# The two ends of a chunked scan: order, loads and engines of its first image and its last unit

## The chip, the cores and the metric

One core of one Trainium2 chip runs the whole program in one launch. The metric is device time in microseconds (us), the median of several executions. The kernel before took 3655.25 us (three runs, 3648.51 to 3655.76).

## What is computed

Two layers on a batch of 32 images with 96 channels of 56 x 56 pixels, all in float32. Layer 0 is a ConvNeXt block: a 7x7 depthwise convolution, layer norm over the channels, a two-layer MLP with GELU, and a residual. Layer 1, the one that the change concerns, is a selective scan along the 3136 pixels of each image:

```python
x = conv5x5_depthwise(x) + conv_b
xs = silu(x).reshape(B, C, L)
dts, Bs, Cs = split(einsum('kd,bdl->bkl', x_proj_w, xs))          # 6, 4, 4 rows
delta = softplus(einsum('dr,brl->bdl', dt_w, dts) + dt_b)
log_dA = maximum(delta * -exp(A_logs), log(1e-9))                 # 4 states per channel
P = exp(cumsum(log_dA))
hs = P * cumsum(delta * Bs * xs / maximum(P, 1e-9))
y = einsum('bdnl,bnl->bdl', hs, Cs) + xs * Ds
```

## The kernel before, in words

The program has four stages that follow each other: the 7x7 convolution, the MLP, the 5x5 convolution (whose result goes to DRAM as `conv2_d`) and the scan. The change is in the scan stage alone (lines 534 to 757).

The scan cuts each image in two chunks of CH = 1568 pixels. A step `k` is one chunk of one image, of which there are 64; two neighbouring images (NI = 2) share a pair `p`, whose tokens `load(p)` (L565) brings in by one DMA. Each step has NG = 3 units: a unit `i` is 32 channels times 4 states, that is 128 partitions of 1568 elements. There are 192 units.

A step's data go this way.

- `delta_in` (L582): TensorE computes the argument of delta for half a chunk, 784 columns. `delta` (L590): ScalarE takes its Softplus. `delta_x` (L596): GpSimd multiplies delta with the tokens. The tile `du` holds both, delta and product, side by side.
- `keep_du` (L601) writes `du` to DRAM (L602), and `spread_du` (L636) reads it back for one unit, each channel repeated on four partitions, into a tile `rep` (L642). SyncE (SP) issues both, as well as `load`.
- `rows_bc`, `rows_out` and `spread` (L604 to L634) make the tiles `bt` and `ct`, B and C of the step on 128 partitions, through TensorE and copies on ScalarE.
- `decay` (L645): three ScalarE activations, L648 (Exp), L649 and L650, turn the delta half of `rep` into the decay. `drive` (L652): GpSimd multiplies the product half by `bt` (L654).
- `scan` (L656): VectorE runs a scan that makes P (L664, out to PSUM), a combined min and multiply (L667), and a second scan for the state `hs` (L671).
- `weigh` (L676): GpSimd keeps the last column for the image's second chunk (L681) and multiplies `hs` by `ct` (L682).
- `gather` (L684): TensorE sums the four states of a channel and adds `xs * Ds` (L688, L695), half a chunk at a time. `store` (L702): ScalarE copies the sum out of PSUM (L705) and issues the output DMA (L706).

Every instruction here is recorded through `pin`, which keeps each engine's work in the order in which the program is written. So the loop at L716 is the schedule: at its index `i` it emits the loads and spreads for later units, the decay of unit i+2, the drive of unit i+1, the scan of unit i, the weighing of unit i-1 and, at every third index, sums and stores of the step that has just ended. The pair's delta work is emitted from the place where `at` is 0 (L738 to L752); for the first pair this is index -8. Softplus and Exp lie in different tables of ScalarE, so each change between them has a table load.

Buffers: 5 `rep` tiles, 4 `du` tiles, 5 `hs` tiles, 3 token tiles, and two pairs of PSUM banks that all matmul results of the stage share.

Of the kernel before, what the change touches and what calls it, by code (L numbers as in the profile page):

```python
# [8 lines left out]
F32 = mybir.dt.float32  # L9
AF = mybir.ActivationFunctionType  # L10
# [4 lines left out]
B, C, H, W = 32, 96, 56, 56  # L15
# [6 lines left out]
N, R = 4, 6  # L22
# [10 lines left out]
CH = 1568  # L33
NI = 2
NCH = L // CH
HT = CH // 2
BK = HT // 2
# [4 lines left out]
DG = C // 3  # L42
NG = 3
# [3 lines left out]
def convnext_then_scan_kernel(  # L47
# [22 lines left out]
    nc = tc.nc  # L70
    pin = tc.keep_in_program_order
# [8 lines left out]
    conv2_d = dram.tile([C, H, B * W], F32, name="conv2_d")  # L80
    du_d = dram.tile([B * NCH, C, 2, CH], F32, name="du_d")
# [30 lines left out]
    dtb_t = column(dtb, C, "dtb_t")  # L112
# [27 lines left out]
    dsm_t = const.tile([C, C], F32, name="dsm_t")  # L140

    with tc.tile_pool(name="prep", bufs=1) as prep, tc.tile_pool(
        name="prep_ps", bufs=1, space=PSUM
# [7 lines left out]
        at = H - 1 - K1 // 2  # L151
# [170 lines left out]
    with tc.tile_pool(name="mlp", bufs=2) as pool, tc.tile_pool(  # L322
        name="mlp_h", bufs=3, space=PSUM
# [95 lines left out]
        parts = groups * 2  # L419
# [19 lines left out]
    with tc.tile_pool(name="c2", bufs=3) as pool, tc.tile_pool(  # L439
        name="c2k", bufs=1  # L440
# [93 lines left out]
    with tc.tile_pool(name="sc", bufs=2) as pool, tc.tile_pool(  # L534
        name="sc_k", bufs=1, space=PSUM
# [7 lines left out]
        steps = B * NCH  # L543
        units = steps * NG
# [10 lines left out]
        HQ = H // NCH  # L555

        def place(k):

            p, i = divmod(k, NI)
            return p // NCH * NI + i, p % NCH  # L560

        def bank_pair(name):
            return psum.tile([128, 2, 512], F32, name=name, tag="bc")

        def load(p):  # L565
            b, q = place(p * NI)
            xt = pool.tile([C, HQ, NI * W], F32, name=f"xs_{p}", tag="xs", bufs=3)
            pin(nc.sync.dma_start(
                xt, conv2_d[:, q * HQ : (q + 1) * HQ, b * W : (b + NI) * W]
            ))  # L570
            xts[p] = xt

        def tokens(k, s, n):

            p, i = divmod(k, NI)
            hh = HQ // n
            return xts[p][:, s * hh : (s + 1) * hh, i * W : (i + 1) * W]

        def half(ps, s):
            return ps[:, s, :BK].rearrange("p (h w) -> p h w", w=W)  # L580

        def delta_in(k, h):  # L582
            pzs[k, h] = bank_pair(f"pz_{k}_{h}")
            for s in range(2):
                pin(nc.tensor.matmul(  # L585
                    half(pzs[k, h][:C], s), lhsT=wd_t, rhs=tokens(k, 2 * h + s, 4),
                    start=True, stop=True,
                ))
# [4 lines left out]
            pin(nc.scalar.activation(o, z, AF.Softplus, bias=dtb_t, scale=1.0))  # L593
            dus[k, h] = du

        def delta_x(k, h):  # L596
            du = dus[k, h]
            d, u = (du[:, i, :].rearrange("p (h w) -> p h w", w=W) for i in range(2))
            pin(nc.gpsimd.tensor_mul(u, d, tokens(k, h, 2)))  # L599

        def keep_du(k, h):  # L601
            pin(nc.sync.dma_start(du_d[k][:, :, h * HT : (h + 1) * HT], dus.pop((k, h))))  # L602

        def rows_bc(k):  # L604

# [15 lines left out]
        def spread(k, kind, h):  # L621

            to, name = ((bts, "bt"), (cts, "ct"))[kind]
            if h == 0:
                to[k] = pool.tile([128, CH], F32, name=f"{name}_{k}", tag=name)
            pk = bank_pair(f"pk_{k}_{kind}_{h}")
            for s in range(2):
                at = 32 * (2 * kind + s)
                rows = slice(at, at + 2 * N)
                pin(nc.tensor.matmul(  # L630
                    pk[:, s, :BK], lhsT=pick_t[rows], rhs=bns[k][rows, h],
                    start=True, stop=True, tile_position=(at, 0),
                ))
            pin(nc.scalar.copy(two(to[k][:, h * HT : (h + 1) * HT]), pk[:, :, :BK]))  # L634

        def spread_du(i):  # L636

            k, g = divmod(i, NG)
            rep = pool.tile([128, 2, CH], F32, name=f"rep_{i}", tag="rep", bufs=5)
            du = du_d[k, g * DG : (g + 1) * DG, :, :]  # L640
            src = bass.AP(du.tensor, du.offset, [du.ap[0], [0, N], [1, 2 * CH]])
            pin(nc.sync.dma_start(rep.rearrange("p i t -> p (i t)"), src))  # L642
            reps[i] = rep

        def decay(i):  # L645

# [29 lines left out]
        def weigh(i):  # L676
            k, g = divmod(i, NG)
            q, col = place(k)[1], k % NI * NG + g
            ht = hss[i]
            if q < NCH - 1:  # L680
                pin(nc.gpsimd.tensor_copy(carry_h[:, col : col + 1], ht[:, CH - 1 : CH]))  # L681
            pin(nc.gpsimd.tensor_mul(ht, ht, cts[k]))  # L682

        def gather(k, h):  # L684

            py = bank_pair(f"py_{k}_{h}")
            for s in range(2):
                pin(nc.tensor.matmul(  # L688
                    half(py[:C], s), lhsT=dsm_t, rhs=tokens(k, 2 * h + s, 4),
                    start=True, stop=False,  # L690
                ))
            for s in range(2):
                cols = slice((2 * h + s) * BK, (2 * h + s + 1) * BK)
                for g in range(NG):
                    pin(nc.tensor.matmul(  # L695
                        py[g * DG : (g + 1) * DG, s, :BK], lhsT=sel_t,
                        rhs=hss[k * NG + g][:, cols], start=False, stop=True,
                        tile_position=(0, g * DG),
                    ))
            pys[k, h] = py  # L700

        def store(k, h):  # L702
            b, q = place(k)
            yt = pool.tile([C, HT], F32, name=f"y_{k}_{h}", tag="y")
            pin(nc.scalar.copy(two(yt), pys.pop((k, h))[:C, :, :BK]))  # L705
            pin(nc.scalar.dma_start(out[b, :, q * CH + h * HT : q * CH + (h + 1) * HT], yt))  # L706
# [9 lines left out]
        for i in range(-12, units + 2):  # L716

            p, at = divmod(i + 8, PER)
            g = i % NG
            if at == 3 and p + 1 < PC:  # L720
                load(p + 1)
            at_unit(i + AHEAD, spread_du)
            if 0 <= p < PC and 2 <= at:
# [6 lines left out]
            if g == 1 and 0 <= (i + 2) // NG < steps:  # L730
# [5 lines left out]
            if g == 2 and 0 <= (i + 4) // NG < steps:  # L736
                rows_bc((i + 4) // NG)
            if 0 <= p < PC and at == 0:  # L738
                for j, h in halves[:2]:
                    delta_in(p * NI + j, h)  # L740
            at_unit(i + 2, decay)
            at_unit(i + 1, drive)
            if g == 2 and 0 <= (i + 4) // NG < steps:
                rows_out((i + 4) // NG)
            if 0 <= p < PC and at == 0:
                for a, (j, h) in enumerate(halves):
                    if a >= 2:
                        delta_in(p * NI + j, h)
                    delta(p * NI + j, h)
            if 0 <= p < PC and 1 <= at <= 4:  # L750
                j, h = halves[at - 1]
                delta_x(p * NI + j, h)  # L752
            at_unit(i, scan)
            if g == 0 and 0 <= after < steps:
                gather(after, 0)
                store(after, 0)
                gather(after, 1)


# [42 lines left out]
```

## Time and profile before

| | |
|---|---|
| median of three runs | 3655.25 us |
| the profiled execution: device time, span | 3655.9 us, 3654.1 us |
| busy: TensorE, VectorE, ScalarE, GpSimd | 3060.6, 2655.5, 2341.0, 1950.5 us |
| first load of tokens issued (L568) | 1856.24 us |
| first scan, second scan, third scan start (L664) | 1896.48, 1913.20, 1922.07 us |
| last scan ends (L671) | 3639.06 us |

Times inside the execution count from the start of its span. A row of the timeline gives the start, the duration, engine and line, the operation, what it writes and reads, and in brackets the idle time of the engine before it with what ended that. "SPq" and "ACTq" are issues of DMAs by SyncE and ScalarE. In the page, the span is cut in 40 slices and each digit is the busy share of an engine in one slice, in tenths. A row of the waits gives engine, line, what it waited for, the microseconds in total, how often, and the longest. "xN" counts instructions.

### The profile page before, as it was taken

The page shows a single profiled execution, that of the slowest core. Times are in us where ns is not written, and L with a number is a line of the kernel's source. Part 1 is how long each engine was busy: PE and PEld are TensorE (multiplying, and loading weights), DVE is VectorE, ACT ScalarE, POOL GpSimd, SP SyncE. Part 2 cuts the span into 40 slices and gives each one's busy share as a digit, 9 for nine tenths or more (in the row PEclk, how much of TensorE's full clock was granted, in tenths as well). Part 3 has the DMA queues.
Part 4 walks back from the last instruction along what each step waited for, and adds up shares of the span by engine and source line. Part 5 has one row for each costly group of instructions (what it writes and reads, how often), then busy time and mean ns, then how long its engine had stood idle before and what let it go on. Part 6 is the DMA issues. An engine that isn't in the chain of part 4 may idle for free. (4 is left out here: it accounts for less than half of the span.)

```text
span 3654.1 us, 46458 instructions
## 1 busy us (share of the span) xinstructions
PE 3060.6 (84%) x17290; PEld 1286.4 (35%) x17290; DVE 2655.5 (73%) x1771; ACT 2341.0 (64%) x2133; POOL 1950.5 (53%) x1241
## 2 busy tenths in 40 slices
PE   7999996899999999899957777777777777777775
PEld 5777774333333333333312222222222222222221
DVE  5666665233333333599949999999999999999998
ACT  3555553333333333577858878888888888888884
POOL 2333332122222222100028999999999999999996
PEclk9999998899999999999966666666666666666666
DMA  5555553455555554699977778877877877878873
GB/s 153 166 167 167 168 168 107 149 162 160 163 163 162 162 160 125 169 281 281 288 232 264 259 253 281 276 257 267 276 260 267 281 245 275 274 244 277 281 258 108
DMA packets 302054, 790.70 MB, mean 216 GB/s; under 512 B 123012, under 2 KB 180164, under 8 KB 277156
## 3 DMA queue, kind: packets, MB, share of 16 engines
q1 hardware_dynamic: 259076, 669.31, 56.7%
q0 software_dynamic: 28416, 79.87, 7.3%
q10 hardware_dynamic: 14336, 38.54, 2.7%
q8 instruction: 137, 2.24, 0.3%
q14 instruction: 89, 0.73, 0.1%
HBM read 551.83 MB, written 235.74 MB: 216 GB/s over the span
## 5 line engine op out<-in xcount | busy, mean ns | idle before, releaser
L682 POOL TENSOR_TENSOR hs<-hs,ct 128x1568 f32<-128x1568 f32 x192 | 673.3, 3507 | 104.8 <-DVE hs L671 93.0
L664 DVE TENSOR_TENSOR_SCAN pv<-rep,pv 128x1568 f32<-128x1568 f32 x192 | 664.5, 3461 | 72.2 <-ACT rep L650 54.2
L654 POOL TENSOR_TENSOR rep<-rep,bt 128x1568 f32<-128x1568 f32 x192 | 674.9, 3515 | 14.6 <-DMA rep<-du_d 14.6
L382 ACT ACTIVATE g<-ph,b1p_t 128x896 f32<-128x896 f32 x336 | 320.5, 1005 | 511.8 <-PE ph L372 511.8
L402 DVE SCALAR_TENSOR_TENSOR o<-po,b2r_t,x 128x224 f32<-128x224 f32 x336 | 190.4, 608 | 572.4 <-PE po L391 572.4
L286 PE MATMUL ps<-xq,wt 120*112 120x448 f32 x1536 | 581.9, 540 | 14.1 <-POOL xq L281 14.1
L414 POOL DMA_DIRECT2D block_d<-o x336 | 183.7, 553 | 703.5 <-DVE o L402 621.3
L286 PEld LDWEIGHTS ps<-xq,wt 120*112 120x112 f32 x1536 | 429.4, 280 | 166.2 <-POOL xq L281 14.3
L372 PE MATMUL ph<-h,w1r_t 32*128 32x448 f32 x4032 | 440.3, 559 | 55.8 <-DVE h L362 54.4
L599 POOL TENSOR_TENSOR du<-du,xs 96x784 f32<-96x784 f32 x128 | 236.3, 1847 | 373.7 <-ACT du L593 373.7
L585 PE MATMUL pz<-xs,wd_t 96*96 96x392 f32 x512 | 277.3, 707 | 172.0 <-ACT du L593 139.1
L391 PE MATMUL po<-g,w_t 128*32 128x448 f32 x4032 | 413.1, 543 | 0.0
L695 PE MATMUL py<-hs,sel_t 128*32 128x392 f32 x1536 | 328.6, 685 | 68.5 <-POOL hs L682 68.5
L630 PE MATMUL pk<-bn,pick_t 8*128 8x392 f32 x1024 | 287.3, 682 | 98.4 <-ACT y L705 78.8
L667 DVE SCALAR_TENSOR_TENSOR pv<-pv,rep 128x1568 f32<-128x1568 f32 x192 | 345.6, 1800 | 21.1 <-POOL hs L682 1.4
L480 PE MATMUL ps<-xq,wt 128*32 128x448 f32 x3072 | 309.9, 548 | 39.3 <-DMA xq<-block_d 36.5
L671 DVE TENSOR_TENSOR_SCAN hs<-rep,carry_h,pv 128x1568 f32<-128x1568 f32 x96 | 334.0, 3479 | 10.4 <-DVE pv L667 0.5
L503 DVE COPY st<-yt 28x896 f32<-28x896 f32 x288 | 317.7, 1103 | 26.9 <-DMA conv_d<-st 13.2
L671 DVE TENSOR_TENSOR_SCAN hs<-rep,pv 128x1568 f32<-128x1568 f32 x96 | 328.4, 3421 | 10.3 <-DVE pv L667 0.9
L688 PE MATMUL py<-xs,dsm_t 96*96 96x392 f32 x512 | 308.6, 746 | 11.7 <-ACT bn L618 6.1
L648 ACT ACTIVATE rep<-rep,a_t 128x1568 f32<-128x1568 f32 x192 | 308.3, 1606 | 11.6 <-DMA rep<-du_d 11.2
L649 ACT ACTIVATE rep<-rep,lift_t 128x1568 f32<-128x1568 f32 x192 | 307.6, 1602 | 6.2
(85 smaller groups left out, 3155.4 us busy)
## 6 DMA issues: line engine op xcount, KB each, us to landing
rep<-du_d SPq DMA_DIRECT2D x192, 1568.0 KB
du_d<-du SPq DMA_DIRECT2D x128, 588.0 KB
xq<-block_d SPq DMA_DIRECT2D x192, 225.0 KB
block_d<-o POOLq DMA_DIRECT2D x336, 120.0 KB, 5.6
xt<-in_x_dram SPq DMA_DIRECT2D x192, 196.0 KB
h<-conv_d SPq DMA_DIRECT2D x84, 448.0 KB
x<-in_x_dram SPq DMA_DIRECT2D x336, 112.0 KB
conv_d<-st SPq DMA_DIRECT2D x96, 392.0 KB
```

What stands on the lines that cost most here:

```text
L286: nc.tensor.matmul(ps[:, j, :PQ].rearrange("p (i r) -> p i r", i=BI), lhsT=wv[:KR, t], rhs=xq[:KR, j, :, t : t + W2], start=(t == 0), stop ...
L372: pin(nc.tensor.matmul(phs[i // 2][:, i % 2, :HALF], lhsT=w1r_t[rows, d, f * 128 : (f + 1) * 128], rhs=hts[n, d][rows, s * HALF : (s + 1) ...
L382: nc.scalar.activation(gt, ph[:, :, :HALF], AF.Gelu, bias=b1p_t[:, f : f + 1], scale=1.0)
L391: pin(nc.tensor.matmul(po[CB * i : CB * i + CB, :HALF], lhsT=w2_t[:, f, CB * d : CB * d + CB], rhs=gts[n, s, f, i // 2][:, i % 2], start=( ...
L480: pin(nc.tensor.matmul(ps[RW * f : RW * f + RW, h, : B * QW].rearrange("p (b q) -> p b q", q=QW), lhsT=wv[:, f, t], rhs=xv[:, :, t : t + Q ...
L503: pin(copy(st[:, :, :, :, f], yt[RW * f : RW * f + QR].rearrange("p h (b q) -> p h b q", q=QW),))
L654: pin(nc.gpsimd.tensor_mul(ut, ut, bts[i // NG]))
L664: pin(nc.vector.tensor_tensor_scan(grown, da, zero, pv[:, last : last + 1] if q else 1.0 / EPS, ALU.mult, ALU.add))
L667: pin(nc.vector.scalar_tensor_tensor(run, in0=grown, scalar=1.0, in1=ut, op0=ALU.min, op1=ALU.mult))
L671: pin(nc.vector.tensor_tensor_scan(ht, da, run, carry_h[:, col : col + 1] if q else 0.0, ALU.mult, ALU.add))
L682: pin(nc.gpsimd.tensor_mul(ht, ht, cts[k]))
L695: pin(nc.tensor.matmul(py[g * DG : (g + 1) * DG, s, :BK], lhsT=sel_t, rhs=hss[k * NG + g][:, cols], start=False, stop=True, tile_position= ...
```

## The change

At the start of the scan, for the first pair:

- The first pair's tokens are loaded by two DMAs, one for each image.
- All that the first image needs is emitted at loop index -8 in an order of its own: a Softplus of one column ahead of everything, delta of both halves, delta alone to DRAM, `rep` of unit 0 with delta alone; after these its product, now on VectorE, to DRAM and into the other half of `rep`; then the load of the second pair, `rep` of units 1 and 2, `bt`, decay and drive of unit 0; then delta, product and store of the second image.
- Decay and drive of unit 1 are emitted at index -2, ahead of the second pair's delta work; decay of unit 2 at index -1.

At the end, for the last unit and the last step:

- The product of `hs` and `ct` is made by VectorE for the first 784 columns and by GpSimd for the others.
- The sums over the first two units, with the `xs * Ds` part, are emitted before the last unit's; only the last unit's matmuls remain after it.
- The second half's copy is made by VectorE and its output DMA is issued by SyncE.

The core of the diff:

```diff
         def load(p):
-            pin(nc.sync.dma_start(
-                xt, conv2_d[:, q * HQ : (q + 1) * HQ, b * W : (b + NI) * W]
-            ))
+            rows = conv2_d[:, q * HQ : (q + 1) * HQ, b * W : (b + NI) * W]
+            for i in range(1 if p else NI):
+                cols = slice(None) if p else slice(i * W, (i + 1) * W)
+                pin(nc.sync.dma_start(xt[:, :, cols], rows[:, :, cols]))
...
-        def delta_x(k, h):
+        def delta_x(k, h, engine=nc.gpsimd):
...
-        def keep_du(k, h):
-            pin(nc.sync.dma_start(du_d[k][:, :, h * HT : (h + 1) * HT], dus.pop((k, h))))
+        def keep_du(k, h, part=slice(0, 2)):
+            pin(nc.sync.dma_start(
+                du_d[k][:, part, h * HT : (h + 1) * HT], dus[k, h][:, part]
+            ))
...
-        def spread_du(i):
+        def spread_du(i, part=slice(0, 2)):
...
-            pin(nc.gpsimd.tensor_mul(ht, ht, cts[k]))
+            if i < units - 1:
+                pin(nc.gpsimd.tensor_mul(ht, ht, cts[k]))
+            else:
+                for engine, cols in (nc.vector, slice(0, HT)), (nc.gpsimd, slice(HT, CH)):
+                    pin(engine.tensor_mul(ht[:, cols], ht[:, cols], cts[k][:, cols]))
...
-        def store(k, h):
+        def store(k, h, copy=nc.scalar.copy, queue=nc.scalar):
...
+            if p == 0 and at == 0:
+                deltas, products = slice(0, 1), slice(1, 2)
+                warm = pool.tile([C, 1], F32, name="warm", bufs=1)
+                pin(nc.scalar.activation(warm, dtb_t, AF.Softplus))
+                for h in range(2):
+                    delta_in(0, h)
+                for h in range(2):
+                    delta(0, h)
+                for h in range(2):
+                    keep_du(0, h, deltas)
+                spread_du(0, deltas)
+                for h in range(2):
+                    delta_x(0, h, nc.vector)
+                    keep_du(0, h, products)
+                rows_bc(0)
+                rows_out(0)
+                spread_du(0, products)
+                load(1)
+                for u in range(1, NG):
+                    spread_du(u)
+                for h in range(2):
+                    spread(0, 0, h)
+                decay(0)
+                drive(0)
+                for h in range(2):
+                    delta_in(1, h)
+                    delta(1, h)
+                    delta_x(1, h)
+                    keep_du(1, h)
+                continue
...
+            ready = {-2: [1], -1: [2], 0: []}.get(i, [i + 2])
+            driven = {-2: [1], -1: [], 0: []}.get(i, [i + 1])
...
+            if i == units - 1:
+                for h in range(2):
+                    gather(steps - 1, h, range(NG - 1))
+            if i == units:
+                for h in range(2):
+                    gather(steps - 1, h, range(NG - 1, NG))
+                store(steps - 1, 0)
+                store(steps - 1, 1, nc.vector.tensor_copy, nc.sync)
```

More of the change, by code (lines that the diff above doesn't have):

```diff
@@ L594, in delta @@
             dus[k, h] = du
-        def delta_x(k, h):
+        def delta_x(k, h, engine=nc.gpsimd):
             du = dus[k, h]
             d, u = (du[:, i, :].rearrange("p (h w) -> p h w", w=W) for i in range(2))
-            pin(nc.gpsimd.tensor_mul(u, d, tokens(k, h, 2)))
-        def keep_du(k, h):
-            pin(nc.sync.dma_start(du_d[k][:, :, h * HT : (h + 1) * HT], dus.pop((k, h))))
+            pin(engine.tensor_mul(u, d, tokens(k, h, 2)))
+        def keep_du(k, h, part=slice(0, 2)):
+            pin(nc.sync.dma_start(
+                du_d[k][:, part, h * HT : (h + 1) * HT], dus[k, h][:, part]
+            ))
         def rows_bc(k):
@@ L634, in spread @@
             pin(nc.scalar.copy(two(to[k][:, h * HT : (h + 1) * HT]), pk[:, :, :BK]))
-        def spread_du(i):
+        def spread_du(i, part=slice(0, 2)):
             k, g = divmod(i, NG)
[L639 to L643, printed above, removed]
+            if i not in reps:
+                reps[i] = pool.tile([128, 2, CH], F32, name=f"rep_{i}", tag="rep", bufs=5)
+            to = reps[i][:, part].rearrange("p i t -> p (i t)")
+            du = du_d[k, g * DG : (g + 1) * DG, part, :]
+            src = bass.AP(du.tensor, du.offset, [du.ap[0], [0, N], [1, to.shape[1]]])
+            pin(nc.sync.dma_start(to, src))
         def decay(i):
@@ L681, in weigh, with gather @@
                 pin(nc.gpsimd.tensor_copy(carry_h[:, col : col + 1], ht[:, CH - 1 : CH]))
[L682 to L691, printed above, removed]
+            if i < units - 1:
[3 more added lines that the diff above has]
+                    pin(engine.tensor_mul(ht[:, cols], ht[:, cols], cts[k][:, cols]))
+        def gather(k, h, parts=range(NG)):
+            if parts[0] == 0:
+                pys[k, h] = bank_pair(f"py_{k}_{h}")
+                for s in range(2):
+                    pin(nc.tensor.matmul(
+                        half(pys[k, h][:C], s), lhsT=dsm_t, rhs=tokens(k, 2 * h + s, 4),
+                        start=True, stop=False,
+                    ))
+            py = pys[k, h]
             for s in range(2):
                 cols = slice((2 * h + s) * BK, (2 * h + s + 1) * BK)
-                for g in range(NG):
+                for g in parts:
                     pin(nc.tensor.matmul(
@@ L699, in gather @@
                     ))
-            pys[k, h] = py
-        def store(k, h):
+        def store(k, h, copy=nc.scalar.copy, queue=nc.scalar):
             b, q = place(k)
             yt = pool.tile([C, HT], F32, name=f"y_{k}_{h}", tag="y")
-            pin(nc.scalar.copy(two(yt), pys.pop((k, h))[:C, :, :BK]))
-            pin(nc.scalar.dma_start(out[b, :, q * CH + h * HT : q * CH + (h + 1) * HT], yt))
+            pin(copy(two(yt), pys.pop((k, h))[:C, :, :BK]))
+            pin(queue.dma_start(out[b, :, q * CH + h * HT : q * CH + (h + 1) * HT], yt))
         def at_unit(i, fn):
@@ L715, in convnext_then_scan_kernel @@
         halves = [(i, h) for i in range(NI) for h in range(2)]
-        for i in range(-12, units + 2):
+        for i in range(-12, units + 1):
             p, at = divmod(i + 8, PER)
             g = i % NG
-            if at == 3 and p + 1 < PC:
+            if p == 0 and at == 0:
[28 more added lines that the diff above has]
+                continue
+            if at == 3 and p + 1 < PC and (p + 1) != 1:
                 load(p + 1)
-            at_unit(i + AHEAD, spread_du)
-            if 0 <= p < PC and 2 <= at:
+            if i + AHEAD >= NG:
+                at_unit(i + AHEAD, spread_du)
+            if 0 < p < PC and 2 <= at:
                 j, h = halves[at - 2]
@@ L729, in convnext_then_scan_kernel @@
                 store(after, 1)
-            if g == 1 and 0 <= (i + 2) // NG < steps:
+            if g == 1 and 0 < (i + 2) // NG < steps:
                 for h in range(2):
@@ L735, in convnext_then_scan_kernel @@
                     spread((i + 1) // NG, 1, h)
-            if g == 2 and 0 <= (i + 4) // NG < steps:
+            if g == 2 and 0 < (i + 4) // NG < steps:
                 rows_bc((i + 4) // NG)
-            if 0 <= p < PC and at == 0:
+            ready = {-2: [1], -1: [2], 0: []}.get(i, [i + 2])
+            driven = {-2: [1], -1: [], 0: []}.get(i, [i + 1])
+            if 0 < p < PC and at == 0 and i != -2:
                 for j, h in halves[:2]:
                     delta_in(p * NI + j, h)
-            at_unit(i + 2, decay)
-            at_unit(i + 1, drive)
-            if g == 2 and 0 <= (i + 4) // NG < steps:
+            for u in ready:
+                if u:
+                    at_unit(u, decay)
+            for u in driven:
+                if u:
+                    at_unit(u, drive)
+            if g == 2 and 0 < (i + 4) // NG < steps:
                 rows_out((i + 4) // NG)
-            if 0 <= p < PC and at == 0:
+            if 0 < p < PC and at == 0:
                 for a, (j, h) in enumerate(halves):
-                    if a >= 2:
+                    if a >= 2 or i == -2:
                         delta_in(p * NI + j, h)
                     delta(p * NI + j, h)
-            if 0 <= p < PC and 1 <= at <= 4:
+            if 0 < p < PC and 1 <= at <= 4:
                 j, h = halves[at - 1]
@@ L753, in convnext_then_scan_kernel @@
             at_unit(i, scan)
-            if g == 0 and 0 <= after < steps:
+            if g == 0 and 0 <= after < steps - 1:
                 gather(after, 0)
```

## The prediction

> **What bounds the kernel now.** I read the page first (busy rows, slices), then the waits of DVE, then the timelines around the scan stage's first and last units, then every L664 start against the end of its decay on L650. Page, parts 1 and 2:
>
> ```profile
> PE 3060.6 (84%) x17290; PEld 1286.4 (35%) x17290; DVE 2655.5 (73%) x1771; ACT 2341.0 (64%) x2133; POOL 1950.5 (53%) x1241
> DVE  5666665233333333599949999999999999999998
> ACT  3555553333333333577858878888888888888884
> POOL 2333332122222222100028999999999999999996
> ```
>
> The whole-span shares mix stages. From slice 21 on, the scan stage, DVE is full, POOL as well, ACT at 8 of 10. The waits of DVE from 1900 us to the end:
>
> ```profile
> DVE pv L664 <- ACT rep L650: 10.4, 4, 7.9
> DVE pv L667 <- POOL hs L682: 1.4, 3, 0.5
> ```
>
> Of 1740 us DVE waits some 12: the stage is a DVE chain of 192 units, about 9.04 us each (1913.20 to 3639.06 for 191). An edit pays only where it starts this chain earlier, avoids a hole in it, or shortens what follows its end. The start, two timelines:
>
> ```profile
> 1856.24 0.31 SPq L568 DMA_DIRECT2D xs<-conv_d  x1
> 1864.23 9.92 PE L585 MATMUL pz<-xs,wd_t 96*96 96x392 f32 x16 [19.06 <-DMA xs<-conv_d]
> 1867.20 1.28 ACT L593 ACT_TABLE_LOAD   x1 [19.14 <-PE pz L585]
> ...
> 1871.36 0.64 SPq L602 DMA_DIRECT2D du_d<-du  x1
> 1872.04 0.61 SPq L568 DMA_DIRECT2D xs<-conv_d  x1
> 1873.15 4.92 SPq L602 DMA_DIRECT2D du_d<-du  x1
> ```
>
> ```profile
> 1883.77 0.55 SPq L642 DMA_DIRECT2D rep<-du_d  x1
> ...
> 1891.58 1.60 ACT L648 ACTIVATE rep<-rep,a_t 128x1568 f32<-128x1568 f32 x1 [11.23 <-DMA rep<-du_d]
> ...
> 1896.46 1.28 ACT L593 ACT_TABLE_LOAD   x1
> 1896.48 3.43 DVE L664 TENSOR_TENSOR_SCAN pv<-rep,pv 128x1568 f32<-128x1568 f32 x1 [43.84 <-ACT rep L650]
> ...
> 1908.30 1.60 ACT L648 ACTIVATE rep<-rep,a_t 128x1568 f32<-128x1568 f32 x1
> ...
> 1913.20 3.43 DVE L664 TENSOR_TENSOR_SCAN pv<-rep,pv 128x1568 f32<-128x1568 f32 x1 [7.92 <-ACT rep L650]
> ```
>
> See two things. The second delta store (1873.15) lies behind the 1.2 MB load of the next pair, so the first rep load leaves only at 1883.77. And ACT puts four Softplus, two ct copies and two table loads between decay 0 and decay 1: 16.7 us from the end of one to the end of the other. The tail:
>
> ```profile
> 3635.58 3.48 DVE L671 TENSOR_TENSOR_SCAN hs<-rep,carry_h,pv 128x1568 f32<-128x1568 f32 x1
> 3639.20 3.48 POOL L682 TENSOR_TENSOR hs<-hs,ct 128x1568 f32<-128x1568 f32 x1 [5.58 <-DVE hs L671]
> 3642.74 2.82 PE L695 MATMUL py<-hs,sel_t 128*32 128x392 f32 x8 [7.55 <-POOL hs L682]
> ...
> 3650.67 0.32 ACTq L706 DMA_DIRECT2D out_dram<-y  x1
> ```
>
> From the last scan's end to the span's end: 3654.1 - 3639.06 = 15.0 us.
>
> **What the Trainium skill says.** (1) "DMA: Bandwidth & Descriptors", Queues, rings and completion order: descriptors of one issuing engine are consumed in ring order. The trace agrees: L602 of 1873.15 waits out the load in front of it (11.1 us is the longest wait of L642 for it). (2) "ScalarE: Activation LUTs", What ACT_TABLE_LOAD costs: 1.283 us, plus a drain of 1.38; the trace shows 1.28 us and no drain of its own. (3) "SBUF — State Buffer", Who interferes with whom: a DVE instruction with two SBUF inputs and a POOL instruction reading SBUF exclude each other, the first keeps the port. The scan reads pv from PSUM, so no scan row shows it; in the first convolution a POOL copy (L281) starts at 301.64, just as DVE's two-input add of 300.65 (1.09 us) ends: it fits.
>
> **Part by part, in the clock of this profile.**
>
> *Load by image.* The load took 8.0 us, its data moving from about 1857.4 to 1863.0 (DMA shares by window). Half the bytes, but the same count of packets at half their size: if a packet's cost is constant, 0 gained; if by bytes, 2.8; a small packet may cost more, so -1. I take 0.6: PE starts at 1863.6. The second half follows, done by about 1869, beside PE work.
>
> *Table load early.* The warm Softplus runs in ACT's idle 19 us; but the second Softplus is set by PE (1869.79, 5.6 after PE's start), so 0 on the path. Deltas end at 1863.6 + 6.5 = 1870.1.
>
> *Deltas ahead.* POOL's product leaves the path, as does the next load. Store of 96x784: priced by the last output store, same size, 3.4 us (3650.67 to 3654.1): 1873.5. Rep load of 0.8 MB: rep 0 took 7.8 us with 2.2 MB (it and the store issued behind); less the 2.4 us fixed part of the xs load that is 5.4, so 2.0 + 2.4 = 4.4, bounds 3.9 and 6: 1878.0. Decay 4.9 (1891.58 to 1896.48): first scan 1882.9, not 1896.48. ACT's copies for bt and its table load are hidden before 1878; without that cover they would cost their excess.
>
> *Products behind.* DVE takes the two products, about 1 us each (96x784; 1.08 for 896 columns on L362), while idle: 0. Two more stores and one more rep load on SP: the stores are issued at 1874 behind the delta rep (its data end near 1877) and land at about 1879.8 (1.6 us of data, 1.2 of completion); the product rep lands 4.4 later at 1884.3, and POOL's drive (3.5) ends at 1888. DVE's L667 waits 1.7 us; unit 0 ends at 1893.3, cost hidden by the next point.
>
> *Load(1) ahead of rep 1.* In SP's ring now stand the product rep (data to 1883.3), load(1) with 5.6 us (its data, as the first load's above), rep 1 with 3.9 us (1.6 MB at the 420 GB/s of the busiest windows), 1.2 us completion: rep 1 lands at 1894. Bounds: 1889 if load(1) could be passed, 1897 if the reps run at the rate of rep 0. This is the new wait; rep 2 and image 1's two stores queue behind it but are needed later. Image 1's two Softplus and two table loads (4.4 us) on ACT end before, at 1887.3. Decay 1 ends 1899; scan 1 at 1899, not 1913.2.
>
> *POOL behind these waits.* Its order is now drive 0, image 1's two products, drive 1, two products of the next pair, then the weighing of unit 0, drive 2. Drive 0 (to 1888) and the two products (1.85 each, to 1891.7) end before rep 1 is there; drive 1 is done at 1897.5, needed by L667 at 1902.4. The weighing waits for ct, whose copies end 10.6 us after decay 1 as they did after decay 0 (1896.46 to the weighing at 1907.12): from 1909.6 it and drive 2 take 7.0, to 1916.6; L667 of unit 2 wants it at 1919.3. Covered by 2.7 us; if scan 2 came earlier than I say, this would be the next limit.
>
> *The Softplus block moves to between decays 1 and 2.* It costs its 16.7 there: scan 2 at 1915.8, not 1922.07: 6.3 left. Then ACT has no lead over DVE. Before, it needed 51.6 us from decay 1's end (1913.16) to decay 7's (1964.78), 4.1 of them waiting (idle before L705 and L634). After, the block without its decay is one more thing in that stretch, 16.7 - 4.9 = 11.8, and there are new waits: bn, its matmuls and bt stand directly ahead of decay 3, and the y and bt copies ahead of decay 6 wait for PE at half clock (0.7 us a matmul). Not in the trace; between 0 and 6, I take 4.2: 51.6 - 4.1 + 11.8 + 4.2 = 63.5. Decay 7 ends at 1899.1 + 63.5 = 1962.6, and unit 7 starts there instead of 1966.72. **Start: 4.1 us earlier**, not 14.
>
> Does ACT hold that? In the trace of before its lead fell to nothing three times (units 43, 139, 151), for instance
>
> ```profile
> 2292.63 3.49 DVE L664 TENSOR_TENSOR_SCAN pv<-rep,pv 128x1568 f32<-128x1568 f32 x1 [0.96 <-ACT rep L650]
> ```
>
> and each time was back at 3.0 to 3.3 us six units later. So no further loss.
>
> *Tail.* Two thirds of the matmuls and all of L688 move ahead, under the last scan. DVE's half product: 0.97 us by the 1.08 of L362; POOL's half: 1.8 (L599's 1.85 at the same width). By the skill they exclude each other; DVE starts 0.05 us earlier, so POOL ends at 3639.06 + 0.1 + 1.0 + 1.8 = +2.9. PE's two matmuls of the second half 1.4 (0.7 each, from 2.82 for four), to +4.4; DVE's copy 1.0 (ACT's takes 0.81), SP's store 3.4: +8.9. **Tail: 15.0 - 8.9 = 6.1 us less**. With no exclusion 6.6; with POOL first 4.8.
>
> Sum: 4.1 + 6.1 = 10.2 us from this execution's own 3655.9: 3645.7. The median shown, 3655.25, is 0.65 less: 3645.0.
>
> **Rivals.**
> A, rep 1 is in time (DMA faster, or less behind it): decay 1 follows the Softplus pair at once, ends at 1892.3, 6.8 us sooner, all the way to unit 7. Start 11, tail 6: 3638. Against it: the packet times above.
> B, the start gives nothing (small packets slow, or ACT's catching up costs 4 us more): the tail alone, 3655.25 - 6.1 = 3649.1. For it: each of the four estimates on this path (packets, store, two reps) has only one row behind it.
> C, slower: ACT becomes the bound for good. The lead is reset to nothing at unit 7; if each pair's Softplus block then outruns ACT's recovery, each of the 31 remaining pairs pays. It decides from 10.2/31 = 0.33 us per pair; at 1 us per pair 3655 + 21 = 3676. For it: ACT at 8 tenths and three bare leads. Against it: the recovery to 3 us, each time.
> That the early path isn't taken at all can be set aside: the order of both programs has the delta store and its rep load ahead of the product, waiting for ACT alone.
>
> **Chances.** The forecast 0.56, A 0.17, B 0.22, C 0.05. Range 3638 to 3652: from A to the tail alone with POOL first and 2 us on top. About 0.2%, 7.3 us, is what a measurement here can tell from no change: faster needs under 3647.9. That is A, most of the forecast and a little of B: 0.71; same 0.25; slower 0.04, C.
>
> **What will show it.** First L664 near 1883 and second near 1899, with a hole before it ended by the rep load; scan 2 near 1916 and unit 7 some 4 us earlier, both released by the decay's last step on ACT; from the last scan's end 8.9 us, POOL's half product starting as DVE's ends. Second scan before 1895 means A; holes ended by ACT at every sixth unit mean C.

## The result

The changed kernel took 3641.78 us (median of 8 runs, 3639.02 to 3648.92), the kernel before, beside it on the same chip, 3653.95 us (8 runs, 3648.51 to 3656.82). The ratio is 0.997, with a 95% interval from 0.9959 to 0.9981: faster by 0.3%, 12.2 us between the medians, 7 to 15 us by the interval. The profiled execution of the changed kernel took 3640.0 us, its span 3638.2 us.

### The profile page after: what moved, and what is told of

Its sections match the earlier page's. It is cut to its first block, busy times and chain, and to the rows that moved or that the text cites. A ratio compares the mean times of both kernels' runs of the same rounds, so it can differ in the third digit from the quotient of the medians.

```text
span 3638.2 us, 46478 instructions
## 1 busy us (share of the span) xinstructions
PE 3049.4 (84%) x17290; PEld 1284.6 (35%) x17290; DVE 2661.9 (73%) x1775; ACT 2345.0 (64%) x2135; POOL 1944.1 (53%) x1239
## 5 line engine op out<-in xcount | busy, mean ns | idle before, releaser
L658 POOL TENSOR_TENSOR rep<-rep,bt 128x1568 f32<-128x1568 f32 x192 | 674.5, 3513 | 381.5 <-DMA rep<-du_d 381.5
L687 POOL TENSOR_TENSOR hs<-hs,ct 128x1568 f32<-128x1568 f32 x191 | 669.4, 3505 | 104.0 <-DVE hs L675 91.0
L668 DVE TENSOR_TENSOR_SCAN pv<-rep,pv 128x1568 f32<-128x1568 f32 x192 | 664.5, 3461 | 47.6 <-ACT rep L654 29.9
L705 PE MATMUL py<-hs,sel_t 128*32 128x392 f32 x1536 | 327.0, 681 | 59.9 <-POOL hs L687 59.7
L671 DVE SCALAR_TENSOR_TENSOR pv<-pv,rep 128x1568 f32<-128x1568 f32 x192 | 345.6, 1800 | 22.2 <-POOL hs L687 1.4
L675 DVE TENSOR_TENSOR_SCAN hs<-rep,carry_h,pv 128x1568 f32<-128x1568 f32 x96 | 334.1, 3480 | 10.8 <-DVE pv L671 0.9
L675 DVE TENSOR_TENSOR_SCAN hs<-rep,pv 128x1568 f32<-128x1568 f32 x96 | 328.4, 3421 | 9.9 <-DVE pv L671 0.5
L652 ACT ACTIVATE rep<-rep,a_t 128x1568 f32<-128x1568 f32 x192 | 308.3, 1606 | 10.0 <-DMA rep<-du_d 9.6
L653 ACT ACTIVATE rep<-rep,lift_t 128x1568 f32<-128x1568 f32 x192 | 307.6, 1602 | 6.2
L654 ACT ACTIVATE rep<-rep,lift_t 128x1568 f32<-128x1568 f32 x192 | 307.6, 1602 | 6.3
```

The lines of the kernel that those rows point to most:

```text
L658: pin(nc.gpsimd.tensor_mul(ut, ut, bts[i // NG]))
L668: pin(nc.vector.tensor_tensor_scan(grown, da, zero, pv[:, last : last + 1] if q else 1.0 / EPS, ALU.mult, ALU.add))
L671: pin(nc.vector.scalar_tensor_tensor(run, in0=grown, scalar=1.0, in1=ut, op0=ALU.min, op1=ALU.mult))
L675: pin(nc.vector.tensor_tensor_scan(ht, da, run, carry_h[:, col : col + 1] if q else 0.0, ALU.mult, ALU.add))
L705: pin(nc.tensor.matmul(py[g * DG : (g + 1) * DG, s, :BK], lhsT=sel_t, rhs=hss[k * NG + g][:, cols], start=False, stop=True, tile_position= ...
```

## The profile after

In the changed kernel the first load of tokens is L571, the stores of delta and product L603, the `rep` loads L647, Softplus L594, the decay L652 to L654, the drive L658, the first scan L668, the combined min and multiply L671, the second scan L675, the product with `ct` L687 and, for the last unit, L690, the last sums L705, the copy of y L714, its DMA L715. The warm Softplus is L734.

The page, busy rows and slices, in the order in which they were shown of before:

```profile
PE 3049.4 (84%) x17290; PEld 1284.6 (35%) x17290; DVE 2661.9 (73%) x1775; ACT 2345.0 (64%) x2135; POOL 1944.1 (53%) x1239
...
DVE  5666665233333333599959999999999999999998
ACT  3555553333333333488868888888888888878884
POOL 2333332122222222100029999999999999999896
```

The work is the same. The 21st digit, the slice in which the scan begins, has gone from 4 to 5 on VectorE and from 5 to 6 on ScalarE, the next from 8 to 9 on GpSimd. Some other digits of ScalarE and GpSimd differ by one as well, in slices whose code is the same, so a slice of 91 us says no more than that. The waits of VectorE from 1900 us to the end:

```profile
DVE pv L668 <- ACT rep L654: 11.8, 6, 7.6
DVE y L714 <- PE py L705: 3.3, 1, 3.3
DVE pv L671 <- POOL hs L687: 1.4, 3, 0.5
```

Waits for the decay add up to 11.8 us in six places, 7.6 of it ahead of the third scan. The chain of 192 units is as unbroken as before. So the time can only have changed ahead of it, in its first units, and behind it. The timeline of the start:

```profile
1850.70 2.11 SPq L571 DMA_DIRECT2D xs<-conv_d  x2
1850.70 1.28 ACT L734 ACT_TABLE_LOAD   x1 [7.70 <-DMA conv_d<-st]
...
1856.45 4.71 PE L586 MATMUL pz<-xs,wd_t 96*96 96x392 f32 x8 [16.51 <-DMA xs<-conv_d]
...
1864.77 0.52 SPq L647 DMA_DIRECT2D rep<-du_d  x1
...
1870.36 1.60 ACT L652 ACTIVATE rep<-rep,a_t 128x1568 f32<-128x1568 f32 x1 [3.01 <-DMA rep<-du_d]
...
1872.46 0.59 SPq L571 DMA_DIRECT2D xs<-conv_d  x1
1873.10 4.94 SPq L647 DMA_DIRECT2D rep<-du_d  x2
...
1875.26 3.43 DVE L668 TENSOR_TENSOR_SCAN pv<-rep,pv 128x1568 f32<-128x1568 f32 x1 [12.15 <-ACT rep L654]
...
1879.92 1.80 DVE L671 SCALAR_TENSOR_TENSOR pv<-pv,rep 128x1568 f32<-128x1568 f32 x1 [1.23 <-POOL rep L658]
...
1886.18 1.60 ACT L652 ACTIVATE rep<-rep,a_t 128x1568 f32<-128x1568 f32 x1 [6.62 <-DMA rep<-du_d]
...
1891.08 3.43 DVE L668 TENSOR_TENSOR_SCAN pv<-rep,pv 128x1568 f32<-128x1568 f32 x1 [5.91 <-ACT rep L654]
...
1907.43 3.43 DVE L668 TENSOR_TENSOR_SCAN pv<-rep,pv 128x1568 f32<-128x1568 f32 x1 [7.57 <-ACT rep L654]
```

Read it from the brackets. ScalarE's second decay (1886.18) stood idle for 6.62 us and was released by the DMA into `rep`: unit 1's copy, issued at 1873.10 behind the second pair's load of 1872.46. That is the new wait. The third scan waits 7.57 us for ScalarE, which has the four Softplus between the second decay and the third. The tail:

```profile
3622.65 3.48 DVE L675 TENSOR_TENSOR_SCAN hs<-rep,carry_h,pv 128x1568 f32<-128x1568 f32 x1
...
3626.16 0.97 DVE L690 TENSOR_TENSOR hs<-hs,ct 128x784 f32<-128x784 f32 x1
3626.27 2.56 POOL L690 TENSOR_TENSOR hs<-hs,ct 128x784 f32<-128x784 f32 x1 [5.59 <-DVE hs L675]
...
3630.48 0.97 DVE L714 COPY y<-py 96x784 f32<-96x784 f32 x1 [3.35 <-PE py L705]
3631.48 0.34 SPq L715 DMA_DIRECT2D out_dram<-y  x1
```

The last scan ends at 3626.13, the last store is issued 5.35 us later, and yet the span ends 12.05 us later, at 3638.2. What fills the rest is not a busy instruction. The line where the program ends shows it (duration in ns as min/median/max, then first start and last start); first the changed kernel, then the kernel before:

```profile
L856 POOLq DRAIN  x3: 34/93/11175, 3626.2 to 3637.9; - x3
L856 SPq DRAIN  x3: 7/7/7, 3634.4 to 3637.7; - x3
```

```profile
L798 POOLq DRAIN  x3: 34/93/12098, 3639.2 to 3653.9; - x3
L798 SPq DRAIN  x3: 7/7/7, 3653.3 to 3653.6; - x3
```

SyncE's first drain stands where its wait for the last store is over. Before, that was 3653.3, and GpSimd's long drain had ended at 3639.2 + 12.1 = 3651.3, hidden. Now the store is over at 3634.4, and GpSimd's drain ends at 3626.2 + 11.2 = 3637.4: it is the last thing to end.

For what follows, the measure is the time from the first load of tokens (the first L571 row and its like), so that what the unchanged stages ahead do drops out. S0, S1, S2, S7 are the starts of the first scan of units 0, 1, 2 and 7; the last two columns are what stands between S7 and the last scan's end, and from there to the span's end.

| profile | load issued at | S0 | S1 | S2 | S7 | S7 to last scan's end | tail |
|---|---|---|---|---|---|---|---|
| before | 1856.24 | 40.23 | 56.95 | 65.83 | 110.48 | 1672.34 | 15.07 |
| after | 1850.70 | 24.56 | 40.38 | 56.74 | 104.25 | 1671.18 | 12.05 |
| tail_only | 1850.89 | 40.44 | 58.22 | 67.10 | 111.76 | 1670.87 | 12.06 |
| start_only | 1850.71 | 24.65 | 40.68 | 56.77 | 104.31 | 1672.79 | 14.37 |
| tail_dve | 1849.77 | 24.26 | 40.22 | 56.50 | 104.03 | 1673.25 | 8.70 |
| rep1_first | 1853.58 | 24.74 | 35.51 | 53.11 | 100.64 | 1671.80 | 12.05 |
| act_more | 1850.42 | 24.92 | 40.94 | 57.30 | 104.87 | 1671.11 | 12.06 |
| old_order | 1852.87 | 25.22 | 52.35 | 61.22 | 105.88 | 1671.09 | 12.07 |
| early_load | 1848.82 | 24.79 | 51.59 | 60.46 | 105.12 | 1672.55 | 9.93 |
| one_load | 1848.55 | 27.28 | 43.64 | 59.65 | 107.15 | 1672.48 | 12.07 |
| both_fixed | 1857.80 | 25.65 | 38.35 | 57.77 | 103.98 | 1672.68 | 10.10 |
| both_fixed_again | 1845.42 | 25.02 | 35.75 | 54.15 | 99.91 | 1670.57 | 8.70 |

The two profiles of before and after differ by 15.9 us of span: 5.5 ahead of the first load, 6.2 from there to S7, 1.2 in the steady part, 3.0 in the tail. The first 5.5 are not the change's. The code ahead is the same in all twelve, and their load leaves anywhere from 1845.4 to 1857.8; with the old start (tail_only) it left at 1850.89, with the new one (start_only) at 1850.71. Likewise the steady part scatters by 2.7 us over these kernels. The other profiles say how steady the two parts are: with the old start S7 is 110.48 and 111.76, with the start of the changed kernel 104.03 to 104.87 in the four profiles that have it (after, start_only, tail_dve, act_more). What the change gave in these two profiles is 6.2 + 3.0 = 9.2 us. The medians are 12.2 us apart; the 3 us more belong to no part measured here, and 9.2 lies within the interval.

## The experiments

Theories for the tail: as forecast (the product, the last sums, the copy and the store set the end), against **the drain** (GpSimd's drain ends some 8.6 us after GpSimd's last product, and the tail cannot be shorter than that). For the start: **DMA order** (unit 1's `rep` waits for the load ahead of it) and **ScalarE** (whatever is won early is kept or lost by ScalarE's work up to unit 7).

### tail_only and start_only: each end by itself

tail_only is the kernel before with the new end alone: the index -8 block and the split load are taken out, the tail's edits stay. start_only is the other half:

```diff
-            if i < units - 1:
-                pin(nc.gpsimd.tensor_mul(ht, ht, cts[k]))
-            else:
-                for engine, cols in (nc.vector, slice(0, HT)), (nc.gpsimd, slice(HT, CH)):
-                    pin(engine.tensor_mul(ht[:, cols], ht[:, cols], cts[k][:, cols]))
+            pin(nc.gpsimd.tensor_mul(ht, ht, cts[k]))
...
-                store(steps - 1, 1, nc.vector.tensor_copy, nc.sync)
```

> The kernel before with the change's end alone. Theory D (after POOL's last product its end-of-program drain runs 8.6 us, and that drain, not the last store, sets the end): from the last scan's end to the span's end 12.1 us as in the changed kernel, 15.0 before, so 3 us faster than before. Theory of the prediction (the chain of product, matmuls, copy and store sets the end): 8.9 us, 6 us faster.

> The kernel before with the change's start alone, the old end. Counted from the issue of the first token load, units 0, 1, 2 and 7 start at 24.6, 40.4, 56.7 and 104.2 us as in the changed kernel (40.2, 57.0, 65.8 and 110.5 before), so 6 us faster than before; tail 15.0. If the 5.5 us by which the changed kernel's scan stage began earlier belong to the change, it is 11 us faster; if they are spread between executions, 6.

tail_only: 3647.39 us (13 runs) beside 3650.69 (33 runs of before), ratio 0.9995 (0.9987 to 1.0003). Its tail is 12.06 us, where the forecast for this step was 8.9. start_only: 3644.41 us (21 runs), ratio 0.9983 (0.9976 to 0.9989), S7 at 104.31, tail 14.37. So most of the gain is the start's. The new end by itself cannot be told from no change by its ratio, although its median is 3.3 us lower and its profile's tail 3.0 us shorter. Taken together, 0.17% and 0.05% by the ratios, some 8 us, or 9.6 us by the medians, they make up the whole change's 0.3% within the intervals.

### tail_dve: the last product on VectorE alone

```diff
-                for engine, cols in (nc.vector, slice(0, HT)), (nc.gpsimd, slice(HT, CH)):
+                for engine, cols in (nc.vector, slice(0, HT)), (nc.vector, slice(HT, CH)):
```

GpSimd's last work is then the product of the unit before the last, 9 us earlier.

> The changed kernel with both halves of the last unit's product on VectorE, so that POOL's last work is the unit before. Theory D: the drain is over before the last store lands; end 8 us after the last scan's end instead of 12.1, 4 us faster than the changed kernel. Rival (SP's own landing and its row of waits set the end): only the second half's earlier product counts (0.7 us), 11.4 us.

Measured: 3639.52 us (5 runs), ratio 0.9969 (0.9956 to 0.9981), tail 8.70 us. Its tail, and its line of the program's end:

```profile
3618.12 3.49 POOL L687 TENSOR_TENSOR hs<-hs,ct 128x1568 f32<-128x1568 f32 x1 [2.12 <-DVE hs L675]
...
3627.08 1.86 DVE L690 TENSOR_TENSOR hs<-hs,ct 128x784 f32<-128x784 f32 x2
...
3632.02 0.34 SPq L715 DMA_DIRECT2D out_dram<-y  x1
```

```profile
L856 POOLq DRAIN  x3: 34/93/12102, 3618.1 to 3635.5; - x3
L856 SPq DRAIN  x3: 7/7/7, 3634.9 to 3635.2; - x3
```

GpSimd's product ended at 3621.61 and its drain at 3630.2, 8.6 us later, as before (3642.68 to 3651.3) and in the changed kernel (3628.83 to 3637.4); in all twelve profiles it is 8.59 us. Now SyncE's wait for the store (3634.9) is last again, and 3.35 us of the tail are gone. The drain theory holds. What GpSimd does in these 8.6 us no run shows. The gain is read from the profile: the ratio, 0.9969, cannot be told from the changed kernel's own 0.997, which was measured in other runs. Beside start_only on the same chip (3644.41 us, tail 14.37) the median is 4.9 us lower.

### rep1_first: unit 1's `rep` ahead of the second pair's load

```diff
                 spread_du(0, products)
+                spread_du(1)
                 load(1)
-                for u in range(1, NG):
-                    spread_du(u)
+                spread_du(2)
```

> The changed kernel with the second pair's load issued after rep 1 instead of ahead of it. Theory of the prediction (rep 1 queued behind that load is the wait at scan 1): rep 1 lands some 5 us sooner, scan 1 starts at 35 us after the first load's issue instead of 40.4, and unit 7 some 4 us sooner (the tokens of the next pair now come 2 us late for its delta); 4 us faster. Rival (the ACT block alone decides, or the load's packets only move the wait to the delta work): scan 1 earlier but unit 7 within 1 us of 104.2, same time.

Measured: 3637.79 us (5 runs), ratio 0.9965 (0.9952 to 0.9977). The decay of unit 1 and its scan:

```profile
1884.19 1.60 ACT L652 ACTIVATE rep<-rep,a_t 128x1568 f32<-128x1568 f32 x1 [1.57 <-DMA rep<-du_d]
1889.10 3.43 DVE L668 TENSOR_TENSOR_SCAN pv<-rep,pv 128x1568 f32<-128x1568 f32 x1 [0.65 <-ACT rep L654]
```

ScalarE waits 1.57 us for the `rep` instead of 6.62, S1 comes 4.9 us sooner, S7 3.6. The order on SyncE's queue was the cause of that wait. This agrees with the Trainium skill, "DMA: Bandwidth & Descriptors", Queues, rings and completion order, which says that each DMA engine takes the descriptors of one issuing engine's ring in their order. Of the 4.9 us, 1.3 are lost again up to S7, most of it at once: the tokens come later, the first of the four Softplus waits 2.84 us for TensorE, and S1 to S2 is 17.6 us instead of 16.4. The ratio does not separate this kernel from the changed one (0.997) either; the gain is read from the profile, and the two profiles of both_fixed below, which have the same order, have S1 at 38.35 and 35.75.

### act_more: 1.5 us more for ScalarE

One extra copy of 128x1568 on ScalarE behind the decay of unit 5.

```diff
+            if i == 3:
+                extra = pool.tile([128, CH], F32, name="extra", bufs=1)
+                pin(nc.scalar.copy(extra, cts[0]))
```

> The changed kernel with one extra ScalarE copy of 128x1568 (1.6 us) after unit 5's decay, into a tile that nobody reads. Theory of the prediction (ScalarE works without a pause from decay 1 to decay 7 and sets unit 7's start): units 0 to 6 as in the changed kernel (unit 6 93 us after the first load's issue), unit 7 at 105.9 instead of 104.2. Rival (POOL, or the tokens' DMAs, set unit 7): 104.2.

One profile: S7 at 104.87, against 104.25. But S0 to S3, ahead of the copy, were late by 0.4 to 0.6 as well, so the copy's 1.48 us cost about 0.1. The expectation missed. In the next Softplus block ScalarE had waits to give back; after first, then with the copy, in each case the third and fourth Softplus and one stretch of the engines (columns: PE, PEld, DVE, ACT and POOL busy us with counts, then the granted TensorE clock, DMA share, GB/s):

```profile
1942.42 0.91 ACT L594 ACTIVATE du<-pz,dtb_t 96x784 f32<-96x784 f32 x1 [2.26 <-POOL rep L658]
1945.04 0.91 ACT L594 ACTIVATE du<-pz,dtb_t 96x784 f32<-96x784 f32 x1 [1.71 <-PE pz L586]
```

```profile
1944.00:1950.00 6.00, 6.00 (x26) 1.73 (x24) 5.79 (x3) 3.79 (x4) 6.00 (x2) 0.50 0.87 245
```

```profile
1943.97 0.91 ACT L594 ACTIVATE du<-pz,dtb_t 96x784 f32<-96x784 f32 x1 [1.55 <-POOL du L600]
1946.32 0.91 ACT L594 ACTIVATE du<-pz,dtb_t 96x784 f32<-96x784 f32 x1 [1.44 <-PE pz L586]
```

```profile
1944.00:1950.00 6.00, 5.81 (x29) 1.71 (x28) 5.79 (x3) 4.29 (x5) 5.94 (x2) 0.78 0.83 234
```

The granted clock was 0.50 in one and 0.78 in the other. The eight matmuls for the third and fourth Softplus, which start when the first Softplus is over, took 5.5 us in the changed kernel and 4.6 us with the copy, so TensorE delivered sooner. Up to unit 7 the chain thus runs through ScalarE and TensorE in turn, and ScalarE's time is not all of it. What the copy would have cost at an equal clock, and whether it had a part in the clock, is not shown; there is one profile of each kernel. That ScalarE alone sets unit 7 is not shown either.

### old_order: the Softplus block ahead of decay 1 again

```diff
-            ready = {-2: [1], -1: [2], 0: []}.get(i, [i + 2])
-            driven = {-2: [1], -1: [], 0: []}.get(i, [i + 1])
-            if 0 < p < PC and at == 0 and i != -2:
+            ready = [i + 2]
+            driven = [i + 1]
+            if 0 < p < PC and at == 0:
...
-                    if a >= 2 or i == -2:
+                    if a >= 2:
```

> The changed kernel with the decays, drives and the next pair's delta matmuls from unit 1 on back in the loop's old order, so that the next pair's four Softplus stand ahead of decay 1 again instead of ahead of decay 2. Theory (only ScalarE's amount of work and the arrival of the next pair's tokens count, not where the Softplus stand): its Softplus start when the tokens have come and their matmul is done, 34.6 us after the first load's issue, scan 1 at 50 instead of 40.4, but no hole at scans 2 and 7, so unit 7 at 104, the same time as the changed kernel. Rival (the order is itself a gain): unit 7 some 6 us later.

Measured: 3644.27 us (10 runs), ratio 0.9978 (0.9969 to 0.9987). S1 is late (52.35), then there is no hole: S1 to S7 53.5 us for six units, which took 63.9 in the changed kernel. At S7 the two orders are 1.6 us apart, 0.7 of which S0 had already (25.22 against 24.56), ahead of the edit. This lies between the two expectations, nearer to the one that the order counts for nothing. So bringing decay 1 ahead of the Softplus block moves the hole from before the second scan to before the third and wins 1.6 us at most, not the 12 by which S1 is earlier.

### early_load: the second pair's load ahead of the product

old_order with tail_dve's end and the load moved up by one place:

```diff
-                spread_du(0, products)
                 load(1)
+                spread_du(0, products)
```

> As old_order, with the second pair's load issued one step earlier, ahead of the product half of rep 0, and the last unit's product on VectorE alone. Theory (with the tokens there, the pair's Softplus follow image 1's at once and share their table load): tokens land 26 us after the first load's issue, scan 1 at 44, unit 7 at 97.5, tail 8.7; 10 us faster than the changed kernel, 3 faster than both_fixed. Rival (product rep behind the load makes drive 0 late, so scan 0 stalls more than it gains): L671 of unit 0 stalls over 6 us and unit 7 is not under 101.

Measured: 3640.79 us (5 runs), ratio 0.9968 (0.9956 to 0.9981), S1 51.59, S7 105.12: a miss, since I expected the second scan near 44. The tokens came in time, but:

```profile
1882.47 1.80 DVE L671 SCALAR_TENSOR_TENSOR pv<-pv,rep 128x1568 f32<-128x1568 f32 x1 [5.43 <-POOL rep L658]
...
1884.27 2.38 SPq L603 DMA_DIRECT2D du_d<-du  x2
...
1888.57 0.91 ACT L594 ACTIVATE du<-pz,dtb_t 96x784 f32<-96x784 f32 x1 [5.62 <-DMA du_d<-du]
```

Unit 0 itself now waits 5.43 us for its drive, since the product half of its `rep` lies behind the tokens. On GpSimd the second image's two products are queued behind that drive (it ended at 1882.4), SyncE stores them from 1884.27 on, and the third Softplus waits 5.62 us for the first of these stores to land, since it writes into one of the four `du` tiles. One late drive thus reaches ScalarE by way of GpSimd, SyncE and a DMA. That is the rival of the expectation, with a stall a little smaller than it named. The tail of 9.93 us, against 8.70 in tail_dve with the same end, is TensorE's; the last 16 sums, first here, then in tail_dve:

```profile
3626.72 4.91 PE L705 MATMUL py<-hs,sel_t 128*32 128x392 f32 x16
```

```profile
3627.19 3.74 PE L705 MATMUL py<-hs,sel_t 128*32 128x392 f32 x16
```

In the 4 us after the last scan the granted clock was 0.56 here and 1.00 in tail_dve.

### one_load: the first tokens in one DMA

```diff
-            for i in range(1 if p else NI):
-                cols = slice(None) if p else slice(i * W, (i + 1) * W)
-                pin(nc.sync.dma_start(xt[:, :, cols], rows[:, :, cols]))
+            pin(nc.sync.dma_start(xt, rows))
```

> The changed kernel with the first pair's tokens in one DMA again; nothing else differs. Theory (the split itself brings the first token products 2.2 us forward, since each image's half lands by itself): PE's first pz 8.0 us after the load is issued instead of 5.75, the first scan 26.8 us after it instead of 24.6, unit 7 at 106.4 instead of 104.25, time about 2 us longer than the changed kernel, near 3644. Rival (the 2.2 us were chance or came from the stage ahead): PE at 5.8, first scan at 24.6, unit 7 at 104.3, and 3642.

Measured: 3644.34 us (20 runs), ratio 0.9983 (0.9977 to 0.999). Its load and first products:

```profile
1848.55 0.31 SPq L569 DMA_DIRECT2D xs<-conv_d  x1
1856.77 4.75 PE L584 MATMUL pz<-xs,wd_t 96*96 96x392 f32 x8 [19.08 <-DMA xs<-conv_d]
```

The products start 8.22 us after the load, S0 is at 27.28 and S7 at 107.15. The split is thus worth 2.5 us at the products and 2.9 at S7, not the 0.6 of the forecast. The other profiles agree: 8.0 to 8.2 us in the three with one load, 5.4 to 6.0 in the nine with two. The end of this kernel, which is that of the changed one, adds something on the drain:

```profile
L854 POOLq DRAIN  x3: 34/102/11180, 3628.3 to 3640.0; - x3
L854 SPq DRAIN  x3: 7/7/7, 3637.5 to 3639.7; - x3
```

At a granted clock of 0.51 behind the last scan its sums were slow and its store was over 9.35 us after the last scan, 1.1 later than in the changed kernel. The tail is 12.07 all the same: GpSimd's drain, to 3628.3 + 11.2 = 3639.5, still ended last.

### both_fixed, twice: rep1_first and tail_dve together

> The two repairs together: rep 1 ahead of the second pair's load, and the last unit's product on VectorE alone. If they are independent, unit 7 at 100.6 and tail 8.7 as each gave alone: 7 us faster than the changed kernel.

> The same kernel as the both_fixed run, once more, in five rounds. Theory that the two repairs add: unit 7 at 100.6 us after the first load, 8.7 to 10.1 us after the last scan, and a median near 3635. Rival, that with the start repaired the tail or the DMA of another execution takes it back as in the first profile: unit 7 at 104, tail 10.1, and a median near 3638.

The first time 3637.93 us (5 runs, 3635.03 to 3646.36), ratio 0.9965 (0.9952 to 0.9977); its profile is of the slowest of the five, with unit 1's `rep` released 33.5 us after the first load (30.6 in rep1_first) and S7 at 103.98, no better than the changed kernel's; its tail is 10.10, with a granted clock of 0.51 in the 4 us after the last scan, as in early_load. The second time, on another chip, 3633.95 us (5 runs, 3626.39 to 3635.89) beside 3650.34 for before (25 runs), ratio 0.9951 (0.9939 to 0.9964). Second time, start and end:

```profile
1876.27 1.60 ACT L652 ACTIVATE rep<-rep,a_t 128x1568 f32<-128x1568 f32 x1 [1.53 <-DMA rep<-du_d]
...
1881.17 3.43 DVE L668 TENSOR_TENSOR_SCAN pv<-rep,pv 128x1568 f32<-128x1568 f32 x1 [0.68 <-ACT rep L654]
```

```profile
3612.43 3.48 DVE L675 TENSOR_TENSOR_SCAN hs<-rep,carry_h,pv 128x1568 f32<-128x1568 f32 x1
...
3620.89 0.34 SPq L715 DMA_DIRECT2D out_dram<-y  x1
```

S7 is at 99.91 and the tail 8.70: in this profile the two repairs add, 4.3 + 3.35 us against the changed kernel's; in the first they did not, and each time it is one profile. This version beats the kernel before in both sets. Against the changed kernel (0.997) it is ahead by 0.05% in one and 0.19% in the other, with intervals that overlap.

## Why the prediction was right, and where it was not

3645.0 was forecast and 3641.78 measured, which is about as far from the forecast as from rival A's 3638; that it was the forecast's way and not A's is read from the second scan, which came 40.38 us after the first load (forecast 42.8, A under 38.8). The sum, 10.2 us, is near the 9.2 us that start and tail gave, but two of its terms were off in opposite directions: the start by 2.1 too little, the tail by 3.1 too much. That they nearly cancel is luck. Of the 3.2 us between forecast and median, 1.3 are the kernel before, whose median was 3655.25 in three runs and 3653.95 in eight; the rest is within the interval.

**Load by image: mis-sized.** 0.6 was taken between bounds of -1 and 2.8; measured 2.2 (8.0 to 5.75 us from load to first product) against before, 2.5 against one_load. The half-size packets cost nearly by their bytes: the last packet of the load ended 7.4 us after its issue with 5376 packets of 224 bytes, 7.1 us with 2688 of 448. The forecast had both cases and chose near the wrong one.

**First scan: right, 2.1 us early.** From the load: forecast 26.7, measured 24.56. By steps, forecast and measured: first product 7.4 and 5.75; both deltas 6.5 and 5.66; store 3.4 and 2.66; rep load 4.5 and 5.59; decay 4.9 and 4.90. The rep load was inside its bounds (3.9 to 6). The deltas' 0.8 us are the execution's: the granted clock in the first 5 us of these matmuls was 0.50 before and 0.62 after, and at 0.50 in three profiles with the new start (old_order and both of both_fixed) they took the 6.46 us of before. The store's 0.7 us are a slip in the price: 3.4 us reached to the end of the span, while that store was over at 3653.33, 2.66 us after its issue.

**Product behind: right.** VectorE waits 1.23 us for the drive of unit 0 (forecast 1.7).

**Load(1) ahead of rep 1: right.** From S0 to S1 16.1 us were forecast, 15.8 measured, and the wait is where it was put. rep1_first shows the cause and its size: 4.9 us, near the 5.6 of data that the forecast gave the load.

**Softplus block between decays 1 and 2: right.** S1 to S2 16.8 forecast, 16.4 measured. old_order shows it from the other side.

**Decay 1 to decay 7: right in size, its cause only in part.** 63.5 forecast, 63.9 measured (1891.05 to 1954.91 for the ends). But act_more shows that the stretch isn't ScalarE's alone, so that the 4.2 us taken for new waits on TensorE at half clock is a number that another execution may change. Of these, 3.2 were found where the forecast put them (2.3 ahead of decay 3, 0.9 ahead of decay 6); another 1.4 came in the second Softplus block, whose waits grew from 3.7 to 5.1 us. S7 was forecast 4.1 us earlier than before and came 6.2 earlier; the difference is what S0 had gained, most of it the split load.

**No further loss: right.** After S7 the waits for the decay are 1.3 us in all (11.8 less 7.6, 0.6 and 2.4 ahead of units 2, 3 and 7). Rival C is out.

**Tail: wrong.** 8.9 us were forecast, 12.05 measured, 6.1 us of gain became 3.0. The steps that were priced are right: GpSimd's half ended at +2.7 (forecast 2.9), with 0.97 us for VectorE's half first and 2.56 for GpSimd's, of which some 0.8 is waiting, if half of its 3.48 us for the whole is the work. This agrees with the Trainium skill, "SBUF — State Buffer", Who interferes with whom, which says that a VectorE instruction with two SBUF inputs and a GpSimd instruction that reads SBUF contend for a shared port; the wait shows as a longer product, not as a later start. The copy ended at +5.3 (forecast 5.4) and the store was over at +8.3, so that without anything else the end would have been near +9.1. Missing was a term: GpSimd's drain at the program's end, 8.6 us past its last product. In the profile of before it could be seen, ending 2.0 us ahead of the store; the forecast took the store for the only thing behind the last scan and did not ask what else ends there. Priced, it gives 2.7 + 8.6 = 11.3, and with the 0.8 us from there to the span's end 12.1.

**Rivals.** A (rep 1 in time) is what rep1_first made; its S7 came 3.6 us earlier, not the 6.8 that were given for it, since `rep` still arrives 1.57 us late and the tokens behind it are later. B (the start gives nothing) is ruled out by start_only.

## What to carry to other kernels

When an edit shortens the end of a program, list all that must end there, each engine's own finish too, and take the latest of the others as the floor; here GpSimd's half of the last product ended 0.9 us sooner than its whole, and only as much could its drain; giving it none of that product took another 3.35 us from the tail. Where one queue serves several consumers, order its transfers by when each is first waited for: the same transfers in another order moved the second scan by 4.9 us in one profile, and by 2.0 and 4.6 in two more. When an early wait is removed, follow the chain until it meets a hole that was there anyway: 12 us at the second scan were at most 1.6 at the eighth.

## What the runs showed of the hardware

- GpSimd's drain at the end of the program ended 8.59 us after its last product in all twelve profiles, whether that product took 2.56 or 3.48 us and whether or not it was in the last unit.
- Loading 1.2 MB as two halves, 5376 packets of 224 bytes instead of 2688 of 448, brought the first half 2.2 to 2.5 us sooner; the whole took 7.3 to 7.6 us to its last packet in nine profiles and 7.1 to 7.2 in three, so twice as many packets, each half as large, cost about 5% more time.
- The TensorE clock granted for the same work differed from one execution to the next: in the 4 us after the last scan it was 1.00 in tail_dve and 0.56 in early_load, and the same 16 matmuls took 3.74 and 4.91 us.
- Code that no kernel changed took 12 us more or less from one profiled execution to the next, as much as the whole effect under study: the parts had to be measured from an event close by.
